# Early query products, key copies and row scaling at the layer boundary of an eight-layer linear-attention stack

## The chip, the cores and the metric

The kernel runs on one core of one Trainium2 chip. The metric is device time in microseconds (us) of one execution. A core has five engines that run their own queues in order and wait for each other through semaphores: PE (matrix products; its weight loads are listed as PEld), DVE (elementwise work with reductions), ACT (activation functions and copies), POOL (elementwise work), and SP (here it issues the weight loads from memory). PE writes its results into eight banks of accumulator memory (PSUM), from which DVE and ACT read.

## The reference

`x` is 512 tokens by 512 features. Three blocks are added to it: cross-attention over 8192 context tokens, a stack of eight linear-attention layers, and an expert layer. All times of this change lie in the stack (about 1234 to 2510 us of the profiled execution). One of its layers, cut to what matters:

```
q = x @ Wq + bq;  k = x @ Wk + bk;  v = x @ Wv + bv
Q = elu(q) + 1;   K = elu(k) + 1
KV = sum over tokens of K * v;   Ksum = sum over tokens of K
V = Q * KV / (Q * Ksum + 1e-6)
x = layernorm(gelu(V @ Wo + bo) + x) * ln1_s + ln1_b
h = gelu(x @ Wf1 + bf1)
x = layernorm(gelu(h @ Wf2 + bf2) + x) * ln2_s + ln2_b
```

Everything is computed in 32-bit floating point.

## The kernel before, in words

**Layout.** The 512 tokens are four tiles of 128 rows (t = 0 to 3). `cur` holds x with tokens on the partitions, `curT` the same with features on the partitions, as the products need it. A layer's queries and values are eight products of 128 features by 512 tokens each (`chunks` 0 to 3 are queries, 4 to 7 values). The keys, like the hidden layer, are computed in a form with seven half products in place of eight (`Seven`); its first two (`p12`) need only the first half of the tokens, `take` reads them from their bank (an ACT copy, L748, and a DVE addition, L749) and hands the first half of the keys to `keys_taken`, which applies elu. `token_sums` (L720 to L723) makes sums of the two halves of the tokens, three on DVE and one on POOL, and `rest` does the other products of the keys (`p5`, `p6`, `p7`, `p4`, `p3`) with DVE additions between (`add6`, L782, is the first, and `p3` reuses the bank that `add6` reads).

**elu.** `elu1` makes elu(x)+1 in five operations: for queries ACT's relu of the negative (L621) and relu (L625), both read from the bank, ACT's exponential (L626), a POOL operation (L627) and DVE's sum (L628). For keys the first is DVE's L623.

**The layer boundary.** The last layernorm of a layer ends tile by tile (`finish`): ACT's gelu, DVE's addition and moments, a root by Newton steps of one column each (L82), and DVE's normalization (L929). Tiles 2 and 3 come last, one closely behind the other. For each tile `turn` transposes the normalized rows on PE (L944) and ACT copies them scaled and shifted into `curT` (L946, four copies of 128x128). `affine` scales and shifts the rows into `cur` (L937, L938), on DVE for tiles 0 and 1 and on POOL for tiles 2 and 3. In the first layer `transpose_into` (L594, L595) takes the place of `turn`.

`features` runs at the start of the next layer, and PE's order in it is written out by hand: the keys' first products and query products 0 and 1 for the first half of the tokens; the transposes of tile 2; query product 2 for the first half; the transposes of tile 3; query products 0 and 1 for tile 2, then for tile 3, and product 2 for the second half; `rest`; and the other five products. The early products 0 to 2 stand in one bank each (`held`), a bank having room for all 512 tokens. `done` hands a product to elu: for the early ones first the half 0 to 255, then the half 256 to 511.

**What sets the order.** PE's order is that of the program text. The other engines' order is made by a scheduler when the program is built, which also places the waits; `tc.issue_after(x)` keeps what is recorded under it behind x in that order. Accesses to one bank by PE and another engine are kept apart by waits even where they touch different columns.

**Rows.** Each layer needs six rows of parameters in copies for all partitions (`row`, loaded by ACT's queue, L986). They stand in nine buffers, so rows 1 and 2 of a layer go where rows 4 and 5 of two layers before stood (the scale and shift of `affine` at the boundary, R_S2 and R_B2), and are loaded a layer early, at that boundary.

Of the kernel before, what the change touches and what calls it, by code (L numbers as in the profile page):

```python
# [11 lines left out]
ALU = mybir.AluOpType  # L12
# [7 lines left out]
T = 512  # L20
# [25 lines left out]
R_BO, R_S1, R_B1, R_BF2, R_S2, R_B2 = range(6)  # L46
# [8 lines left out]
def perceiver_kernel(  # L55
# [3 lines left out]
    nc = tc.nc  # L59
# [58 lines left out]
    def normalize(dst, src, n, eps, roots=None):  # L118
        mv, r = roots or (moments(src, n), None)
        if r is None:  # L120
            r = rsqrt_of(mv[:, :, 1], n, eps)
        for i in range(n):
            last = nc.vector.tensor_scalar(
                dst[:, i, :], src[:, i, :], mv[:, i, 0:1], r[:, i : i + 1], ALU.subtract, ALU.mult
            )
        return last
# [204 lines left out]
    while min(met) < NCHUNK:  # L331
        p = k % NPAIR
# [192 lines left out]
    last = -1  # L525
    for u, n in enumerate(size):
# [6 lines left out]
        for i in range(n):  # L533
            d = end[u] + 1 + i * span // n // 2
            at(d, late_exponentials if d in end[-3:] else exponentials, u, i)
            last = max(d + 1, first)
# [32 lines left out]
    def attention_weights(l):  # L569
        return [weights(big, m[l], f"{n}{l}") for m, n in ((wk, "wk"), (wq, "wq"), (wv, "wv"), (wo, "wo"))]  # L570
# [19 lines left out]
    def transpose_into(dst, src, t, space, tag):  # L590

        pt = space.tile([P, DC, P], F32, tag=tag, name="pt")
        for dc in range(DC):
            nc.tensor.transpose(pt[:, dc, :], src[:, dc * P : (dc + 1) * P], ident)  # L594
        return nc.scalar.copy(dst[:, :, t * P : (t + 1) * P], pt)  # L595

    with ExitStack() as s_:
# [9 lines left out]
        H = T // 2  # L607
# [23 lines left out]
        def feature(ps, w, c0, xT, t0=0, n=T):  # L631
            for dc in range(DC):
                nc.tensor.matmul(  # L633
                    ps[:, t0 : t0 + n], w[:, dc, c0 : c0 + P], xT[:, dc, t0 : t0 + n],
                    start=(dc == 0), stop=(dc == DC - 1),
                )

        def features(k7, chunks, xT, turns, done, normed):

            held = {}

            def product(i, t0=0, n=T):
                if t0 == 0:
                    held[i] = mm.tile([P, T], F32, tag="mm", name="ps")
                feature(held[i], *chunks[i], xT, t0, n)

            if 1 in turns:
                for p in range(2):  # L650
                    k7.p12(p, 0, P, False)
                turns[1]()
                product(0, 0, P)
                for p in range(2):
                    k7.p12(p, P, P, False)
                product(0, P, P)
            else:
                for p in range(2):
                    k7.p12(p, 0, H, False)
                product(0, 0, H)  # L660
            product(1, 0, H)
            turns[2]()
            with tc.issue_after(normed.ins) if normed else nullcontext():
                for p in range(2):
                    k7.take(p)
            product(2, 0, H)
            turned = turns[3]()
            for t in range(2):
                k7.token_sums(t)
            with tc.issue_after(turned.ins):  # L670
                for i in range(3):
                    done(i, held[i], 0, H)
            for t in (2, 3):
                for i in range(2):
                    product(i, t * P, P)
            product(2, H, H)
            with tc.issue_after(turned.ins):
                for i in range(3):
                    done(i, held[i], H, H)
            k7.rest((0, 1))  # L680
            for i in range(3, len(chunks)):
                product(i)
                done(i, held[i], 0, T)
# [230 lines left out]
        def finish(ps, old, bias, t, eng, g=None):  # L914

            if g is None:
                g = gpool.tile([P, D], F32, tag="g", name="g")
                nc.vector.tensor_tensor(g, ps, bias, ALU.add)
            nc.scalar.activation(g, g, AF.Gelu_apprx_tanh)  # L919
            nc.vector.tensor_tensor(g, g, old[:, t, :], ALU.add)  # L920
            mv = small.tile([P, 1, 2], F32, tag="mv1", name="mv")
            st = small.tile([P, 6], F32, tag="st", name="st")
            nc.vector.bn_stats(st, g)
            nc.vector.bn_aggr(mv[:, 0, :], st)
            r = rsqrt_of(mv[:, :, 1], 1, 1e-6)
            if eng is None:
                return g, mv[:, 0, 0:1], r
            if eng is nc.vector:
                last = nc.vector.tensor_scalar(g, g, mv[:, 0, 0:1], r, ALU.subtract, ALU.mult)  # L929
            else:  # L930
                n = small.tile([P, 1], F32, tag="nmr1", name="nmr")
                last = nc.vector.scalar_tensor_tensor(n, mv[:, 0, 0:1], -1.0, r, ALU.mult, ALU.mult)
                nc.scalar.activation(g, g, AF.Identity, bias=n, scale=r)
            return g, last

        def affine(dst, g, scale, shift, eng=nc.vector):
            eng.tensor_tensor(dst, g, scale, ALU.mult)  # L937
            eng.tensor_tensor(dst, dst, shift, ALU.add)  # L938

        def turn(dst, g, t, c_scale, c_shift):  # L940

            pt = acc.tile([P, DC, P], F32, tag="acc", name="pt")
            for dc in range(DC):
                nc.tensor.transpose(pt[:, dc, :], g[:, dc * P : (dc + 1) * P], ident)  # L944
            for dc in range(DC):
                last = nc.scalar.activation(  # L946
                    dst[:, dc, t * P : (t + 1) * P], pt[:, dc, :], AF.Identity,
                    bias=col[:, c_shift + dc : c_shift + dc + 1], scale=col[:, c_scale + dc : c_scale + dc + 1],
                )
            return last  # L950
# [11 lines left out]
        cur = cpl.tile([P, TT, D], F32, tag="cur", name="cur0")  # L962
        curT = cpl.tile([P, DC, T], F32, tag="curT", name="curT0")
        last = None
        for t in range(TT):
            with tc.issue_after(last.ins) if t else nullcontext():
                last = normalize(cur[:, t : t + 1], x_sb[:, t : t + 1], 1, 1e-5, rooted.get(t))
        s_.enter_context(tc.manual_schedule(engines={nc.tensor.engine}))
        transpose_into(curT, cur[:, 0, :], 0, acc, "acc")
        turns = {t: lambda dst=curT, src=cur[:, t, :], t=t: transpose_into(dst, src, t, acc, "acc") for t in (1, 2, 3)}  # L970

        def keys_of_layer(w_k, xT):

            sw = [hpool.tile([P, 2, 2, P], F32, tag="h", name="sw") for _ in range(4)]
            k7 = Seven([(w_k, ac * P) for ac in range(DC)], xT, sw, None, None, None)
            for p in range(2):
                k7.weight_sums(p, (1, 2, 3, 4))
            return k7

        for l in range(NL):  # L980
            w_k, w_q, w_v, w_o = ahead if l else first[0]
            w_1, w_2 = hidden_weights(l) if l else first[1]
            row = []
# [71 lines left out]
            k7 = k7 if l else keys_of_layer(w_k, curT)  # L1055
            k7.sx = [hpool.tile([P, 2, H], F32, tag="h", name="sx") for _ in range(4)]
            k7.tiles, k7.out = keys_tiles, keys_taken
            features(k7, [(w, ac * P) for w in (w_q, w_v) for ac in range(DC)], curT, turns, taken, last if l else None)


# [3 lines left out]
            gs = {}  # L1064
# [9 lines left out]
            turns = {t: lambda dst=midT, g=gs[t], t=t, c=c1: turn(dst, g, t, *c) for t in (1, 2, 3)}  # L1074
# [54 lines left out]
            for p in range(2, NF // 2):  # L1129
# [13 lines left out]
                last = s7.p4(p)  # L1143
# [12 lines left out]
            def next_sums(t):  # L1156
                def f(q):
                    if q + 4 < back.N:
                        back.token_sums(t, q + 4)
                    elif t == 0 and l + 1 < NL:  # L1160
                        back.token_sums(2, q + 4 - back.N)
                return f

            cur = cpl.tile([P, TT, D], F32, tag="cur", name="cur")
# [11 lines left out]
            for t in (0, 2):  # L1176
                if t:
                    ahead = attention_weights(l + 1)
                g = back.products(t, row[R_BF2], between if t else lambda q: None, next_sums(t))
                for i in range(2):  # L1180
                    gs[t + i], last = finish(None, mid, None, t + i, nc.vector, g[i])
                with tc.issue_after(last.ins):
                    for i in (1, 0) if t else (0, 1):
                        affine(cur[:, t + i, :], gs[t + i], row[R_S2], row[R_B2], nc.gpsimd if t else nc.vector)
            turns = {t: lambda dst=curT, g=gs[t], t=t, c=c2: turn(dst, g, t, *c) for t in (2, 3)}
            k7 = made[0]

# [266 lines left out]
```

## Time and profile before

| what | us |
|---|---|
| median of three runs (lowest, highest) | 2622.29 (2621.86, 2625.03) |
| the profiled execution | 2622.8 |
| its span (first to last instruction) | 2621.0 |
| PE busy | 2510.6 |
| DVE, POOL, ACT busy | 1767.2, 1416.8, 1199.8 |
| early query products of a boundary restart (L633), seven boundaries | 1413.16, 1577.76, 1741.99, 1906.03, 2069.98, 2233.89, 2397.86 |

A line of the timeline has the start and the duration, the engine, the source line, the operation, output<-input by the program's names, the shape and a count, and in brackets the idle time before it with what ended it. In a list of waits a line says who waited, for whom, the total, the number of times and the longest. "PEclk", or the granted clock, is the share of PE's full clock that the chip granted. Engines overlap: an engine's busy time is no part of a sum, and only what PE waits for, or does slower, sets the end where PE is busy 96% of the span.

### The profile page before, as it was taken

To read this page: it belongs to the slowest core of one execution; us is meant where nothing else is said; L and a number is where in the kernel's file an instruction comes from. 1 tells how busy PE (TensorE), PEld (TensorE's weight loads), DVE (VectorE), ACT (ScalarE), POOL (GpSimd) and SP (SyncE) were. 2 spreads that over 40 slices of the span, in tenths; PEclk is the share of its full clock that TensorE was granted. 3 is DMA by queue.
4 is the path that set the end of the run, shared out by engine and by line. 5 is a ranking of instruction groups with operands and counts; after the bars stand their busy time and mean duration, and the time that the engine had idled before them with its cause. 6 is when DMAs were issued, how large, how long until landed. Compare 5 with 4: busy or idle time off the path is not lost.

```text
span 2621.0 us, 32785 instructions
## 1 busy us (share of the span) xinstructions
PE 2510.6 (96%) x10936; PEld 1508.8 (58%) x10936; DVE 1767.2 (67%) x3786; ACT 1199.8 (46%) x2263; POOL 1416.8 (54%) x1606
## 2 busy tenths in 40 slices
PE   8999999999999999988999999999999999899998
PEld 4433333433433343334687786877868778587763
DVE  4466767767777677886666676676766767667664
ACT  3466656656666566662514416244162441624413
POOL 0255656665666656763365554655546555475512
PEclk9999999999999999999999999999999999999999
DMA  4111011111111111101423232232322323222235
GB/s 136 46 43 46 26 39 41 41 41 41 41 41 41 37 36 41 29 20 61 164 73 109 78 100 77 73 109 73 104 77 73 109 72 106 77 73 97 65 118 189
DMA packets 98377, 187.43 MB, mean 72 GB/s; under 512 B 10336, under 2 KB 10464, under 8 KB 98208
## 3 DMA queue, kind: packets, MB, share of 16 engines
q1 hardware_dynamic: 88496, 167.29, 20.0%
q10 hardware_dynamic: 8688, 15.94, 1.8%
q0 software_dynamic: 1024, 2.10, 0.2%
q8 instruction: 87, 1.43, 0.2%
q14 instruction: 82, 0.67, 0.1%
HBM read 162.22 MB, written 1.05 MB: 62 GB/s over the span
## 4 chain that ended last, share of the span: by engine, by line
PE 76%; DVE 11%; ACT 6%; issue 4%; POOL 2%; DMA 1%; SPq 0%; DVEq 0%; POOLq 0%; ACTq 0%
PE pb L862 14%; PE pw L727 11%; PE ps L633 7%; PE pv L259 7%; PE ps L727 7%; PE pk L230 7%; PE po L455 7%; PE pc L374 6%; PE po L1070 4%; DVE sc L434 3%; ACT sc L377 2%; ACT sc L435 1%; PE pt L218 1%; PE pf L956 1%; DVE mx L383 1%
## 5 line engine op out<-in xcount | busy, mean ns | idle before, releaser
L445 POOL TENSOR_TENSOR es<-es,sc 128x1024 f32<-128x1024 f32 x222 | 525.3, 2366 | 113.2 <-ACT sc L435 102.3
L383 DVE TENSOR_TENSOR mx<-pc,mx 128x512 f32<-128x512 f32 x448 | 283.0, 683 | 192.2 <-ACT sc L377 192.0
L435 ACT ACTIVATE sc<-sc 128x1024 f32<-128x1024 f32 x272 | 288.1, 1063 | 242.7 <-DVE sc L434 231.6
L377 ACT COPY sc<-pc 128x512 f32<-128x512 f32 x544 | 284.4, 599 | 91.4 <-PE pc L374 78.1
L434 DVE TENSOR_TENSOR sc<-sc,mbc 128x1024 f32<-128x1024 f32 x272 | 319.0, 1207 | 3.7 <-PE mbc L411 2.2
L374 PE MATMUL pc<-qT,k 64*128 64x512 f32 x1088 | 288.2, 621 | 2.9 <-ACT v L265 1.3
L455 PE MATMUL po<-sc,v 128*64 128x512 f32 x1088 | 265.1, 608 | 0.2 <-DVE mx L383 0.2
L230 PE MATMUL pk<-xn,wkv 128*128 128x512 f32 x544 | 253.0, 609 | 7.1 <-ACT v L265 2.9
L259 PE MATMUL pv<-wkv,xn 128*128 128x512 f32 x544 | 249.6, 602 | 6.3 <-DVE sin L241 3.3
L374 PEld LDWEIGHTS pc<-qT,k 64*128 64x128 f32 x1088 | 101.0, 186 | 183.9 <-issue 77.9
L1081 ACT ACTIVATE h<-h,col 128x256 f32<-128x256 f32 x192 | 103.8, 575 | 220.5 <-DVE h L795 151.0
L919 ACT ACTIVATE g<-g 128x512 f32<-128x512 f32 x64 | 39.8, 628 | 319.6 <-DVE g L879 218.8
L230 PEld LDWEIGHTS pk<-xn,wkv 128*128 128x128 f32 x544 | 99.8, 192 | 149.1 <-issue 107.0
L259 PEld LDWEIGHTS pv<-wkv,xn 128*128 128x128 f32 x544 | 98.4, 190 | 140.8 <-issue 106.7
L727 PE MATMUL pw<-curT,cur 128*128 128x256 f32 (+1 forms) x896 | 177.2, 350 | 0.0
L633 PE MATMUL ps<-curT,wq 128*128 128x128 f32 (+2 forms) x584 | 130.5, 386 | 45.0 <-ACT r L625 45.0
L627 POOL TENSOR_SCALAR m<-m 128x256 f32<-128x256 f32 (+1 forms) x104 | 106.5, 1034 | 117.3 <-ACT m L626 115.1
L714 POOL TENSOR_TENSOR cur<-w 128x256 f32<-128x256 f32 x128 | 93.5, 741 | 135.2 <-DVE g L920 84.8
L727 PEld LDWEIGHTS pw<-curT,cur 128*128 128x128 f32 x896 | 150.2, 190 | 16.8 <-DVE curT L720 0.2
L828 POOL TENSOR_TENSOR sh<-h 128x128 f32<-128x128 f32 x120 | 82.8, 690 | 133.1 <-PE pb L862 128.8
L455 PEld LDWEIGHTS po<-sc,v 128*64 128x64 f32 x1088 | 67.8, 137 | 145.9 <-issue 123.5
L633 PEld LDWEIGHTS ps<-curT,wq 128*128 128x128 f32 x584 | 101.0, 220 | 64.6 <-ACT r L625 47.1
(252 smaller groups left out, 4712.9 us busy)
## 6 DMA issues: line engine op xcount, KB each, us to landing
w<-in_wf SPq DMA_DIRECT2D x64, 1024.0 KB, 5.2
k<-cos SPq DMA_DIRECT2D x272, 64.0 KB, 2.0
cb<-in_cx SPq DMA_DIRECT2D x62, 256.0 KB, 3.2
row<-in_rows ACTq DMA_DIRECT2D x48, 256.0 KB, 4.7
f<-in_f SPq DMA_DIRECT2D x10, 1024.0 KB, 5.5
tg<-in_trig SPq DMA_DIRECT2D x16, 512.0 KB, 3.9
wk<-in_wk SPq DMA_DIRECT2D x8, 1024.0 KB, 5.1
wq<-in_wq SPq DMA_DIRECT2D x8, 1024.0 KB, 5.3
```

The costliest lines, as they stand in the source:

```text
L230: nc.tensor.matmul(pk, wkv[:, 0, dc, j * P : (j + 1) * P], xT[b, dc], start=(dc == 0), stop=(dc == DC - 1))
L259: nc.tensor.matmul(pv, xT[b, dc][:, t * P : (t + 1) * P], wkv[:, 1, dc, :], start=(dc == 0), stop=(dc == DC - 1))
L374: nc.tensor.matmul(pc[h], k_sb[b, p][hs, o : o + P], qT[hs, p, :], start=True, stop=True)
L377: copied[0] = nc.scalar.copy(sc[:, h, :], pc[h])
L383: behind[0] = nc.vector.tensor_tensor(mx[u][:, h, :], pc[h], mx[u][:, h, :], ALU.max)
L434: nc.vector.tensor_tensor(sc, sc, mbc[u], ALU.subtract)
L435: nc.scalar.activation(sc, sc, AF.Exp)
L445: nc.gpsimd.tensor_tensor(es[u], es[u], sc, ALU.add)
L455: nc.tensor.matmul(po[u][h * HD : (h + 1) * HD, :], v_sb[b, p][:, t * P + h * HD : t * P + (h + 1) * HD], scores[u, i][:, h, :], start=(i ...
L633: nc.tensor.matmul(ps[:, t0 : t0 + n], w[:, dc, c0 : c0 + P], xT[:, dc, t0 : t0 + n], start=(dc == 0), stop=(dc == DC - 1),)
L727: nc.tensor.matmul(ps, lhs[:, k], rhs[:, k], start=(k == 0), stop=(k == 1))
L862: nc.tensor.matmul(ps[i], lhs, rhs, start=(q == 0 and i in (1, 2, 6, 5, 4)), stop=(q == self.N - 1 and i in (1, 2, 7, 3, 4)),)
```

## The change

Three edits, two in `features` and one where the layers call `affine` (with `affine` now returning its last operation):

1. Query products 0 to 2 go to elu once, over all 512 tokens, when all their products are recorded, and no more in two halves.
2. The keys' `take` is recorded under `issue_after` of the third tile's last copy into `curT`, so that these copies come first.
3. The scaling of each pair of tiles is chained: the first `affine` stands behind the normalization of the second tile of the pair, and each further one behind the one before it, so that POOL takes tile 3, then tile 2.

```diff
@@ features
             product(1, 0, H)
-            turns[2]()
+            turned = turns[2]()
             with tc.issue_after(normed.ins) if normed else nullcontext():
-                for p in range(2):
-                    k7.take(p)
+                with tc.issue_after(turned.ins):
+                    for p in range(2):
+                        k7.take(p)
             product(2, 0, H)
             turned = turns[3]()
             for t in range(2):
                 k7.token_sums(t)
-            with tc.issue_after(turned.ins):
-                for i in range(3):
-                    done(i, held[i], 0, H)
             for t in (2, 3):
                 for i in range(2):
                     product(i, t * P, P)
             product(2, H, H)
+
             with tc.issue_after(turned.ins):
                 for i in range(3):
-                    done(i, held[i], H, H)
+                    done(i, held[i], 0, T)
@@ affine
             eng.tensor_tensor(dst, g, scale, ALU.mult)
-            eng.tensor_tensor(dst, dst, shift, ALU.add)
+            return eng.tensor_tensor(dst, dst, shift, ALU.add)
@@ the layers
                     gs[t + i], last = finish(None, mid, None, t + i, nc.vector, g[i])
-                with tc.issue_after(last.ins):
-                    for i in (1, 0) if t else (0, 1):
-                        affine(cur[:, t + i, :], gs[t + i], row[R_S2], row[R_B2], nc.gpsimd if t else nc.vector)
+                scaled = last
+                for i in (1, 0) if t else (0, 1):
+                    with tc.issue_after(scaled.ins):
+                        scaled = affine(
+                            cur[:, t + i, :], gs[t + i], row[R_S2], row[R_B2], nc.gpsimd if t else nc.vector
+                        )
```

In the built program PE's and SP's instructions stand in the same order as before. On ACT, at a boundary, the order after the gelus was: the two bank copies L748, the first key's relu, tile 2's copies, the table load and the keys' exponentials, tile 3's copies, then the queries' elus in six parts, with the loads of rows 1 and 2 between them. It is now: tile 2's copies, the first bank copy, the load of row 1, the first key's relu, the second bank copy, the table load and the keys' exponentials, tile 3's copies, the load of row 2, then the queries' elus in three parts. The load of row 1 waits for POOL's multiplication of tile 2's rows (L937). At the last boundary there are no rows left to load; there ACT takes both bank copies and the first of tile 3's four copies before the first relu.

## The prediction

> **What bounds the kernel now.** I read the page's busy table first, then what the matmul engine (PE) waits for in the layers (1250 to 2560 us), then the timeline of one layer boundary, then the granted clock over that boundary.
>
> ```profile
> PE 2510.6 (96%) x10936; PEld 1508.8 (58%) x10936; DVE 1767.2 (67%) x3786; ACT 1199.8 (46%) x2263; POOL 1416.8 (54%) x1606
> ```
> ```profile
> PE ps L633 <- ACT r L625: 45.0, 9, 6.2
> PE pt L944 <- ACT g L933: 5.5, 8, 0.7
> PE pt L944 <- DVE g L929: 1.9, 7, 0.3
> ```
>
> PE is the bound: in the eight layers it waits 52 us in all, and 45.0 of them at one place, the early query products (L633) behind the relu that reads their bank (L625): seven boundaries of 6.16 us, and 1.9 us at the first layer's start. The timeline between layers 1 and 2:
>
> ```profile
> 1567.47 1.28 POOL L937 TENSOR_TENSOR cur<-g,row 128x512 f32<-128x512 f32 x1 [12.84 <-DVE g L929]
> 1567.56 1.21 DVE L82 SCALAR_TENSOR_TENSOR ny<-nt,ny 128x1 f32<-128x1 f32 x1
> 1568.80 1.31 DVE L82 SCALAR_TENSOR_TENSOR nt<-ny,vh 128x1 f32<-128x1 f32 x1
> 1568.34 0.60 PE L944 MATMUL pt<-ident,g 128*128 128x128 f32 x4
> 1570.94 0.66 PE L944 MATMUL pt<-ident,g 128*128 128x128 f32 x4 [0.28 <-DVE g L929]
> 1571.25 0.51 ACT L625 ACTIVATE r<-kf,col 128x256 f32<-128x256 f32 x1 [5.79 <-DVE kf L749]
> 1571.67 1.49 ACT L946 ACTIVATE curT<-pt,col 128x128 f32<-128x128 f32 x4
> 1573.17 1.28 ACT L626 ACT_TABLE_LOAD   x1
> 1575.49 1.48 ACT L946 ACTIVATE curT<-pt,col 128x128 f32<-128x128 f32 x4
> 1577.22 0.48 ACT L625 ACTIVATE r<-ps,col 128x256 f32<-128x256 f32 x1
> 1577.76 7.29 PE L633 MATMUL ps<-curT,wq 128*128 128x128 f32 x40 [6.16 <-ACT r L625]
> ```
> ```profile
> 1571.17:1574.58 3.41, 0.43 (x4) 1.00 0.00 0
> 1574.58:1578.00 3.42, 0.24 (x1) 0.50 0.00 0
> 1578.00:1581.41 3.41, 3.41 (x17) 0.50 0.06 20
> 1581.41:1584.82 3.41, 3.41 (x25) 1.00 0.45 136
> ```
>
> Three things are to be seen. The third tile's transposes end at 1568.94, yet its copies (L946) start at 1571.67: ACT stands at a relu that waits for DVE. Two one-column DVE operations take 1.21 and 1.31 us, exactly while POOL's 1.28 us scaling runs (the same operations take 0.16 and 0.22 without it). And the stall is dearer than its 6.16 us: in the last table (stretch; length, PE busy, granted clock) the clock is halved one mostly idle window of 3.41 us later and is whole again only at 1581.41, so PE works 3.65 us at half rate and loses 1.8. Over the seven boundaries that half-rate work is 4.40, 3.65, 3.26, 3.06, 2.95, 2.88 and 6.16 us, so 13.2 us are lost beside the stalls.
>
> **The change, part by part** (times of this boundary, line numbers of before; the built order of each engine's instructions is read from the two programs).
>
> PE's order and SP's are unchanged. *The bank read once*: the products for the third and fourth tile wait only for the copies of curT. *Scaling after the norm*: POOL starts when the fourth tile is normalized; DVE's two operations fall to 0.38 together, so L929 ends 1.21+1.31-0.38 = 2.14 us earlier, at 1568.76. PE's gap before the transposes goes; they end near 1570.9. *Copies ahead*: L946 of the third tile runs 1568.97 to 1570.46, so its 16 products (0.118 each at full clock: 32 took 3.79 in layer 0) run 1570.9 to 1572.8.
>
> The fourth tile sets the rest. The change moves the load of a row (`row`, L986) on ACT's queue ahead of the first relu, and it now waits for POOL's multiplication of the third tile, which POOL does after the fourth tile's two operations. Behind it on ACT stand both keys' elus and, after them, the fourth tile's copies, for which PE waits. That such a wait blocks ACT shows at 1552.70: ACT was idle 15.22 us, issued this load once DVE's L879 was done, and copied 0.44 us later. POOL: three operations of 1.28 with 0.05 to 0.08 between, from 1568.84, end at 1572.8. DVE's token sums beside them are not seen together in this trace; nearest, POOL's 256-wide L722 takes 0.78 to 0.99 beside DVE's L720 instead of L714's 0.73. So 0 to 0.84 (two sums of 0.42) is added; I take 0.5: 1573.3. Then load 0.44, relu 0.42, copy 0.37, table 1.30, exponential, relu and exponential 1.02, four copies 1.5: 5.05 us. The last copy ends at 1578.4 (1576.97 before), the first at 1577.4, and PE idles 4.6 us instead of 6.16. After the last copy PE needs 10 products of 0.12 and 8 of 0.215, so the keys' remaining products start at 1581.35 at full clock; before, 1577.76+3.79+1.72 = 1583.27. **1.9 us at each of six boundaries: -11.4.**
>
> The Trainium skill (SBUF — State Buffer, Who interferes with whom) calls the port pair of VectorE and GpSimd an exclusive lock: who starts first holds it for the whole instruction. By that rule both sums would hold POOL up, 0.84, and the sum would be 2 us worse; the 1.21 and 1.31 us rows agree with the lock.
>
> *The clock.* 4.6 us of idling still holds a window that is idle enough: windows with 1.46 us or less of work are followed by a halved one, windows with 1.73 or more are not (one of 2.10 excepted). By phase, PE then works 2.9 to 6.3 us at half rate, of which 0.3 hides behind copies that it awaits: 1.2 to 2.85 us per boundary. I take 2.2, so 13 for six, where before lost 10.1: **+3** (-3 to +7).
>
> *The last boundary* has no row to load. ACT is not held; the table load ends at 1573.6, the second exponential waits for POOL's port until 1574.7, the copies end at 1576.2, the rest starts at 1579.1: -4.2. PE idles 2.4 us, which halves the clock in some 6 phases of 10, for 1.5: 0.9 instead of 3.1. **-6.4.**
>
> *The first layer's start*: no POOL scaling and no row in the way; both waits (1.42 and 0.47) and their pipeline refill go, and the rest starts at 1253.6 instead of 1255.79: **-2.2.**
>
> *At nothing*: three elus of 512 columns for six of 256. They end later: with 1.3 to 1.5 us for POOL's 512 columns and 0.75 for DVE's, the third query is out at 1587.1 and DVE's L782 pair at 1587.85; PE asks for that bank at 1588.2. Cover 0.35 us, and whatever exceeds it is paid at each boundary. The exponentials for the output product had 3.5 us to spare (y ready 1606.7, asked for at 1610.3); they come 2.3 us earlier, PE 3 at most. The first two tiles' scalings, now one after the other on DVE, lie beside products that run to 1561. cur, later on POOL, is first read at 1615.7.
>
> Sum, on the profiled execution's own 2622.8 us (1.8 outside its span; 0.5 above the median of the runs): 2622.8 - 2.2 - 11.4 + 3 - 6.4 = **2605.8 us**.
>
> **Rivals.**
>
> *The clock takes it back* (0.16). Successive boundaries lie 164.2, 164.0, 163.95 and 163.9 us apart, close to 48 windows of 3.413 = 163.84: whoever arrives early waits longer for the next edge. If the period locks there again, six periods bring 6 x 0.28 = 1.7, the start and the first boundary 4.1, the last 5: 2612. For it: an idle time of 4.6 leaves room for the 5 to 6 us at half rate that this needs. Against: a period without its half-rate loss is 162.4 now (164.23 - 1.82) and would be 160.5; a period of 163.84 then needs 6.7 us at half rate, and at most 6.3 fit. With 0.5 us less gained per layer it fits. The Trainium skill (TensorE: Matmul & The Clock Gate, What's actually happening) has a free-running window of 3413 ns, which these rows show.
>
> *The gate no longer closes* (0.07). If POOL and DVE do not collide and the phases are kind, the half-rate loss of 13.9 goes: 2592. Against: 4.6 us is far over one window.
>
> *The wait only moves* (0.12): the fourth tile's copies come 1.9 us later than I say, PE's gap keeps its length with another releaser: some 2620, the first start alone gained.
>
> *Slower* (0.11): POOL. Its 128-wide L828 went from 0.46 to 0.90 us beside DVE's two-input additions (1549 to 1552). If its 512-wide operations double too, to 2.5, the awaited one ends at 1576.5, the last copy at 1581.6, the rest starts at 1584.6: 1.3 late, with some 8 us of idling and 1.2 more at half rate. Six times 2.5, less some 3 for the first start and the last boundary: 2635. It decides from 2.2 us per operation (0.94 over 1.28, three operations, six boundaries: 17 us). Against: these operations took 1.26 to 1.29 us beside L749 and L623, which waited instead.
>
> **Numbers.** Forecast 0.54, its own range 2598 to 2612 from POOL's 0 to 0.84 and the clock's bounds. Faster is 0.54+0.16+0.07 = 0.77, within 0.2% (5 us, about what a measurement here can tell from none) 0.12, slower 0.11. 2593 to 2621 leaves out the slower rival, most of the open gate and the far side of the wait that only moves.
>
> **What would show it.** Right: L633 waits for curT (L946) and not for L625; no one-column L82 over 1 us at a boundary; the fourth tile's L937 first on POOL; ACT idle before its row load until POOL's third operation; query elus 128x512; 4 to 5 us of idling at six boundaries and about 2.4 at the last. Wrong: POOL's scalings over 2 us, a new wait of PE for DVE's L782, or no ACT wait at the load (then faster still).

## The result, and the profile after

The changed kernel takes 2604.37 us (median of four runs, 2603.30 to 2604.95) beside 2622.47 for the kernel before (four runs, 2621.86 to 2625.03): a ratio of 0.9929, 95% interval 0.9911 to 0.9946. The profiled execution took 2604.4 us with a span of 2602.6; the forecast was 2605.8, from 2593 to 2621. From here on lines of `after` are meant where nothing else is said: one less than in the kernel before up to `affine` and behind it (L945 is the copy into `curT` that was L946, L985 the row load that was L986). In the experiments they shift by a few more.

The page's busy table, and what PE waits for in the layers (1250 to 2560 us):

```profile
PE 2513.4 (97%) x10936; PEld 1513.2 (58%) x10936; DVE 1746.6 (67%) x3762; ACT 1187.6 (46%) x2191; POOL 1413.3 (54%) x1582
```
```profile
PE ps L633 <- ACT curT L945: 27.0, 7, 4.1
PE pt L943 <- ACT g L932: 5.5, 8, 0.7
```

The wait for the relu that reads the bank (45.0 us) is gone; in its place PE waits for the fourth tile's copies, 4.1 us at six boundaries and 2.4 at the last, 27.0 in all. The timeline of the same boundary as before, between layers 1 and 2:

```profile
1564.91 0.55 DVE L928 TENSOR_SCALAR g<-g,mv,ny 128x512 f32<-128x512 f32 x1
...
1565.54 1.30 POOL L936 TENSOR_TENSOR cur<-g,row 128x512 f32<-128x512 f32 x1 [14.06 <-DVE g L928]
1565.69 1.50 ACT L945 ACTIVATE curT<-pt,col 128x128 f32<-128x128 f32 x4 [6.01 <-PE pt L943]
...
1566.92 1.33 POOL L937 TENSOR_TENSOR cur<-cur,row 128x512 f32<-128x512 f32 x1
...
1567.22 1.31 DVE L720 TENSOR_TENSOR sx<-curT,sx 128x256 f32<-128x256 f32 x1
...
1568.21 1.48 POOL L936 TENSOR_TENSOR cur<-g,row 128x512 f32<-128x512 f32 x1
1568.45 0.41 DVE L748 TENSOR_TENSOR kf<-kf,ps 128x256 f32<-128x256 f32 x1
1568.78 1.19 DVE L722 TENSOR_TENSOR sx<-curT,sx 128x256 f32<-128x256 f32 x1
1569.72 0.33 ACTq L985 DMA_DIRECT2D row<-in_rows  x1
...
1570.10 0.51 ACT L625 ACTIVATE r<-kf,col 128x256 f32<-128x256 f32 x1 [2.65 <-DVE sx L722]
...
1570.88 1.28 ACT L626 ACT_TABLE_LOAD   x1
...
1573.20 1.48 ACT L945 ACTIVATE curT<-pt,col 128x128 f32<-128x128 f32 x4
...
1573.70 6.66 PE L633 MATMUL ps<-curT,wq 128*128 128x128 f32 x24 [4.09 <-ACT curT L945]
```

Three things are to be seen. The third tile's copies now come first on ACT (1565.69), as the change says. Then ACT stands idle for 2.65 us. The list names DVE's token sum as releaser, but the row load was issued at 1569.72, 0.03 us after POOL's third scaling ended (1568.21 + 1.48), and the relu follows 0.38 later; the addition for which the relu itself waits (L748) was done at 1568.86. And behind the relu stand the table load, the exponentials and only then the fourth tile's copies, at 1573.20.

The granted clock around two successive boundaries (stretch; length, PE busy, granted clock):

```profile
1569.44:1572.85 3.41, 0.16 (x2) 1.00 0.22 77
1572.85:1576.26 3.41, 2.56 (x12) 0.50 0.33 77
1576.26:1579.67 3.41, 3.41 (x12) 0.50 0.00 0
```
```profile
1733.28:1736.69 3.41, 0.16 (x1) 1.00 0.32 110
1736.69:1740.10 3.41, 3.41 (x17) 0.50 0.15 49
1740.10:1743.51 3.41, 3.41 (x17) 1.00 0.00 0
```

In both a nearly idle window is followed by a halved one. Where PE restarts 0.85 us into the halved window, that window is busy for 2.56 us only and a second halved one follows; where it restarts just ahead of it, the window is full and the clock returns after one. In the kernel before, the clock stayed halved behind a halved window with 2.75 us of work (2397.19 to 2400.61) and returned behind one with 2.88 (2233.35 to 2236.77). The six boundaries take turns: one window, two, one, two, one, two.

PE's instructions are the same in both kernels, so the same instruction's start can be compared from end to end. After minus before, in us:

```
ahead of the stack                +1.73
behind the first layer's start    -0.40   (-2.13)
behind boundaries 1 to 6          -3.29  -4.70  -7.14  -8.33  -10.65  -11.81   (-11.41)
behind the last boundary          -17.02  (-5.21)
end of PE's work                  -17.93  (-0.91)
```

The +1.73 arises ahead of the stack, in cross-attention, which the change does not touch: 0.7 of it in the first 16 us, and 1.3 because after has a halved stretch of 6.83 us (at 316.7) and before one of 3.41 (at 376.5). The -0.91 lies behind the stack; its cause was not followed.

### The profile page after: what moved, and what is told of

Its sections match the earlier page's. It is cut to its first block, busy times and chain, and to the rows that moved or that the text cites. A ratio compares the mean times of both kernels' runs of the same rounds, so it can differ in the third digit from the quotient of the medians.

```text
span 2602.6 us, 32659 instructions
## 1 busy us (share of the span) xinstructions
PE 2513.4 (97%) x10936; PEld 1513.2 (58%) x10936; DVE 1746.6 (67%) x3762; ACT 1187.6 (46%) x2191; POOL 1413.3 (54%) x1582
## 4 chain that ended last, share of the span: by engine, by line
PE 71%; DVE 9%; POOL 7%; issue 7%; ACT 5%; DMA 0%; ACTq 0%; SPq 0%; POOLq 0%; DVEq 0%
PE pw L726 11%; PE pb L861 9%; PE ps L633 7%; PE ps L726 7%; PE pv L259 7%; PE pk L230 6%; PE po L455 6%; PE pc L374 6%; DVE sc L434 4%; PE po L1069 4%; ACT sc L377 2%; ACT sc L435 1%; POOL es L445 1%; PE pt L218 1%; PE pf L955 1%
## 5 line engine op out<-in xcount | busy, mean ns | idle before, releaser
L627 POOL TENSOR_SCALAR m<-m 128x512 f32<-128x512 f32 (+1 forms) x80 | 102.0, 1287 | 75.9 <-ACT m L626 75.1
L861 PE MATMUL pb<-tw,sh 128*128 128x256 f32 x540 | 136.3, 380 | 0.0
```

The costliest lines, as they stand in the source:

```text
L861: nc.tensor.matmul(ps[i], lhs, rhs, start=(q == 0 and i in (1, 2, 6, 5, 4)), stop=(q == self.N - 1 and i in (1, 2, 7, 3, 4)),)
```

## Experiments

All times are medians of four runs (ten for part 3 alone) beside the kernel before on the same chip (2620.9 to 2622.1 in these comparisons); brackets hold the ratio to the kernel before with its 95% interval. The changed kernel's 2604.37 stood beside 2622.47, so a difference from it carries up to 1.5 us of that. The parts of the change are called 1 (banks read once), 2 (third tile's copies ahead of the keys' take) and 3 (scalings chained).

**One part, and all but one.** Part 1 alone (in the kernel before):

```diff
-            with tc.issue_after(turned.ins):
-                for i in range(3):
-                    done(i, held[i], 0, H)
...
-                    done(i, held[i], H, H)
+                    done(i, held[i], 0, T)
```

> The kernel before with one part of the change: the three early queries are read once, behind all products that fill their banks. The third tile's copies stay where they were, between the first key's relu and the table load, and POOL's scalings are not held back. Theory A (what is left of PE's stall in the changed kernel, 4.1 us at six boundaries, is made by ACT standing at the load of a row that waits for POOL's third scaling): here that load stands behind the fourth tile's copies, so these end where they ended before, 1.0 us earlier than in the changed kernel on one scale; PE waits twice, some 1.6 and 1.4 us, and a boundary gains 3.4 us against before: 2622.5 - 2.2 - 7 x 3.4 = about 2597, less up to 10 us if two short waits no longer halve the clock. Theory B (all three parts are needed, the earlier transposes above all): 2606 to 2615. That the bank is not the cause: 2620.

Measured: 2585.19 (0.9858, 0.9843 to 0.9872). One part alone gives twice the gain of the three together. From its list of PE's waits:

```profile
PE ps L633 <- ACT curT L943: 13.7, 14, 1.4
```

PE waits twice per boundary, for the third and the fourth tile's copies, never over 1.4 us, and no window at a boundary is halved. Theory B falls. Theory A fits, with more gain than the 2597 named first, as the clock's part came in full; but this run alone does not tell the load from the order of the copies. The load is also not where it was expected: at the second boundary it stands at 1567.13, ahead of the fourth tile's copies (1568.08), but the scaling for which it waits had ended at 1564.86, and ACT goes on without a gap.

Part 2 left out (of the changed kernel):

```diff
-                with tc.issue_after(turned.ins):
-                    for p in range(2):
-                        k7.take(p)
+                for p in range(2):
+                    k7.take(p)
```

> The changed kernel without the second part: the keys are taken as soon as the fourth tile of the layer below is normalized, and not behind the third tile's copies; banks read once, scalings in a chain as in the changed kernel. ACT's order is then relu, third tile's copies, table load, exponentials, fourth tile's copies, with no load of a row ahead of them. Theory A: the ACT queue is freed from POOL, the fourth tile's copies end 2 to 3 us earlier than in the changed kernel, and the stall of 4.1 us falls below 2.5: 2588 to 2598. Theory B (the copies ahead are what shortens the stall): slower than the changed kernel's 2604.4, some 2606 to 2612.

Measured: 2579.06 (0.9837, 0.9822 to 0.9851), 25 us faster than the changed kernel. Theory B falls; theory A has the direction and too small a size, as its range ended at 2588. From its timeline, ACT at the same boundary, and PE:

```profile
1561.75 0.51 ACT L625 ACTIVATE r<-kf,col 128x256 f32<-128x256 f32 x1 [3.66 <-DVE kf L747]
...
1562.16 1.49 ACT L944 ACTIVATE curT<-pt,col 128x128 f32<-128x128 f32 x4
...
1563.67 1.28 ACT L626 ACT_TABLE_LOAD   x1
...
1565.44 0.33 ACTq L984 DMA_DIRECT2D row<-in_rows  x1
...
1565.99 1.48 ACT L944 ACTIVATE curT<-pt,col 128x128 f32<-128x128 f32 x4
1566.48 4.16 PE L633 MATMUL ps<-curT,wq 128*128 128x128 f32 x24 [0.96 <-ACT curT L944]
```

The relu sets the third tile's copies back by some 0.4 us, which PE does not feel, as it is still at the third query and the fourth tile's transposes. The row load is not ahead of the relu. It stands between the second relu and the last exponential, still ahead of the fourth tile's copies, and costs nothing there: that exponential starts 0.39 us behind its relu, as in the kernel before (0.40).

Part 3 left out (the scalings as before, 1 and 2 as in the change):

> The first two parts of the change without the third: banks read once, third tile's copies ahead of the keys' elus, but the scalings as in the kernel before (first the third tile, as soon as it is normalized). Theory (part two is what costs, through two loads of rows on ACT's queue that wait for POOL and through DVE, where token sums now stand ahead of the key's addition; part three only eases both): in this order the loads stand ahead of the third tile's copies and wait for POOL's scaling of the fourth tile, so PE waits in two places, some 3.5 us more per boundary than with the bank alone (2585), and a halved clock comes back: 2608 to 2620, slower than the changed kernel. Rival (the three parts are nearly independent, part two costs 25 and part three brings 6): 2610. Rival (part two is only bad together with the chain on POOL, which makes its load wait for the third operation and not for the first): 2585 to 2592.

Measured: 2609.82 (0.9955, 0.9940 to 0.9970). From its timeline:

```profile
1571.59 0.33 ACTq L985 DMA_DIRECT2D row<-in_rows  x1
...
1571.98 1.15 ACT L945 ACTIVATE curT<-pt,col 128x128 f32<-128x128 f32 x3 [9.72 <-POOL cur L936]
```

One load stands ahead of the third tile's copies, as expected, the other ahead of the last of them, but both the theory and the rival of independent parts allow this time; only the rival that part 2 harms through the chain alone falls.

Part 3 alone:

> The kernel before with the third part alone: POOL scales the last two tiles one after the other, the fourth first, from when the fourth is normalized; queries still read from their banks in two halves, with PE's products for the last tiles behind the first reading. Theory (two things set a boundary: the bank, and how soon the fourth tile and the keys get through DVE): DVE's two one-column operations fall from 1.21 and 1.31 to 0.2 us, transposes and key additions come 1 to 2 us earlier, ACT's chain with them, and the stall of 6.16 us stays near 5 to 6 at an earlier place: 2608 to 2614. Rival (with the bank still in the way the chain brings nothing, or the keys' token sums beside POOL take it back): 2618 to 2624.

Measured: 2622.91 (1.0003, 0.9994 to 1.0013): nothing. The theory falls and the rival holds. From its timeline:

```profile
1577.52 1.83 POOL L627 TENSOR_SCALAR m<-m 128x256 f32<-128x256 f32 x2
...
1579.22 0.47 ACT L621 ACTIVATE m<-ps,ncol 128x256 f32<-128x256 f32 x1 [1.87 <-DVE kf L628]
...
1580.12 7.45 PE L633 MATMUL ps<-curT,wq 128*128 128x128 f32 x40 [6.50 <-ACT r L625]
```

The transposes do come earlier, but POOL's part of the keys' elu (L627) stands behind the four chained scalings, and the first reading of a query's bank (L621) waits for the keys' sums behind it, as it writes one of the two buffers of `m` that the keys' elus still hold. What DVE gained is lost on POOL, and PE idles 6.50 us instead of 6.16.

So part 1 brings 36 us (2621 to 2585); part 3 nothing without it and 6 with it (to 2579, intervals that just overlap); part 2 costs 25 in both cases (2585.2 to 2609.8, 2579.1 to 2604.4). Part 2 was not run without part 1.

**Why part 2 costs.** The row loads first. They are needed only a layer later, so they can be issued well behind the boundary (changed kernel; `weighed_last` is the last exponential of `weighed` in the layer before):

```diff
-                nc.scalar.dma_start(out=rt, in_=rows[l, i].partition_broadcast(P))
+                with tc.issue_after(weighed_last.ins) if l > 1 else nullcontext():
+                    nc.scalar.dma_start(out=rt, in_=rows[l, i].partition_broadcast(P))
```

> The changed kernel with the loads of the rows for layer l+1 issued only behind the last exponential of layer l's keys' weighing (they are read 100 us and more later), so that ACT meets no load that waits for POOL ahead of the first key's relu. Nothing else differs. Theory A: ACT goes on when the first key is added up (1568.86 at the second boundary) and not when POOL is done (1569.7); copies of the fourth tile 1.2 us earlier, stall 2.9 instead of 4.1: 6 x 1.2 = 7.4 less, and up to 7 more from the clock: 2590 to 2598. Rival (DVE's key additions, stretched by POOL, set the relu; the load only waited beside them): 2602 to 2605. Rival (the clock's windows hold the period at 47 and 48 windows in turn and take the gain back): 2602 to 2605 with a shorter stall but more work at half rate.

Measured: 2590.16 (0.9878, 0.9861 to 0.9894), 14.2 less than the changed kernel. Theory A holds, and the gain stays: the clock did not take it back. Its timeline:

```profile
1562.98 0.74 DVE L748 TENSOR_TENSOR kf<-kf,ps 128x256 f32<-128x256 f32 x2
1563.43 0.51 ACT L625 ACTIVATE r<-kf,col 128x256 f32<-128x256 f32 x1 [0.56 <-DVE kf L748]
...
1566.77 5.41 PE L633 MATMUL ps<-curT,wq 128*128 128x128 f32 x22 [2.38 <-ACT curT L945]
```

ACT now waits 0.56 us for the keys' addition in place of 2.65; PE's stall is 2.4 us, and each of boundaries 2 to 6 has one halved window, the first and the last none. Next, DVE's token sums behind the keys' additions, on top of this:

> The changed kernel with the row loads later (as in the run with that change alone, 2590) and, besides, DVE's token sums of the first and third tile behind the two additions of the keys. The third tile's copies are still ahead of the keys' elus. Theory A (what is left between 2590 and the 2579 of the kernel without the copies ahead is DVE's order: two or three token sums, stretched to 1.2 to 1.3 us each beside POOL, stand ahead of the key's addition for which ACT's relu waits): PE's wait falls from 2.4 to about 1, no halved window, 2578 to 2582. Rival (the order on ACT itself, four copies of 1.5 us ahead of relu and table load, sets it): 2588 to 2591, with a wait of 2.4 us that stays.

Measured: 2587.78 (0.9869, 0.9854 to 0.9883), 2.4 less, with overlapping intervals; PE's stall is 2.2 us. Theory A falls and the rival, whose range began at 2588, holds: what is left is ACT's own order, which the last experiment of this section changes. ACT in this run:

```profile
1562.27 1.50 ACT L947 ACTIVATE curT<-pt,col 128x128 f32<-128x128 f32 x4 [6.00 <-PE pt L945]
...
1564.52 0.91 ACT L625 ACTIVATE r<-kf,col 128x256 f32<-128x256 f32 x2 [0.22 <-DVE kf L749]
1565.45 1.28 ACT L626 ACT_TABLE_LOAD   x1
...
1567.87 1.49 ACT L947 ACTIVATE curT<-pt,col 128x128 f32<-128x128 f32 x4
```

ACT has hardly a gap here. Copies, relus, table load and exponentials follow each other, and the last copies come when all that is done.

**The clock by itself.** The stall filled with useless work (changed kernel, layers 1 to 7; not shown: `product` also keeps the bank that it already has):

```diff
             for t in (2, 3):
                 for i in range(2):
                     product(i, t * P, P)
+                if t == 2 and normed:
+                    for _ in range(2):
+                        product(2, 0, H)
```

> The changed kernel with useless work for PE in the stall: at the seven boundaries the first half of the third query's product (1.72 us) is computed twice more, with the same result, between the products of the third tile and those of the fourth. PE's order is otherwise the same, and 3.44 of the 4.1 us idle are filled. Theory of the clock (a window of 3.41 us that is mostly idle halves the clock for one or two windows): no halved window is left at the boundaries, and the half-rate work of the six boundaries (3.41, 5.98, 3.41, 5.80, 3.41, 5.75, in sum 27.8 us) and of the last (3.41) loses nothing: 13.9 + 1.7 saved, 1.0 paid at the last boundary, whose stall is only 2.42: 2604.4 - 14.6 = about 2590. Rival (the halving comes from something else at a boundary, or returns as power is drawn): 2604 to 2606.

Measured: 2591.99 (0.9882, 0.9867 to 0.9897), 12.4 less than the changed kernel although PE does 24 us more work (seven times 3.44). From its timeline, the third tile's products with the useless ones behind them, and the fourth tile's:

```profile
1566.70 5.41 PE L633 MATMUL ps<-curT,wq 128*128 128x128 f32 x32
1572.77 4.15 PE L633 MATMUL ps<-curT,wq 128*128 128x128 f32 x24 [0.66 <-ACT curT L948]
```

The fourth tile's products take 4.15 us in place of 6.66, and no boundary has a halved window. The theory of the clock holds; 2.2 us of the 14.6 expected did not show. By the starts of the same instructions, each of the six boundaries gained 0.3 to 0.5 us less than expected and the last some 0.5 more; why stays open.

**Towards a better kernel.** From the 2579 kernel, work moved into its last waits (halves of the keys' fifth and sixth product computed early):

> The best kernel so far (no copies ahead, 2579) with work moved into PE's last two waits of a boundary: of the keys' products with sums, the halves that need only the first and third tile's token sums are computed early, those of the fifth product between the third and the fourth tile's query products, those of the sixth behind the third query; the second halves follow. Each 256-wide product becomes two of 128. Theory (PE is the bound, and its waits of 0.96 for the fourth tile's copies and 0.63 for DVE's token sums are all that is left at a boundary): up to 1.4 us at each of seven boundaries and some at the first layer: 2569 to 2574. Rival (the fourth tile's copies only come later relative to the work, or ACT's next elus become the wait, as q's banks are read later): 2576 to 2582.

Measured: 2577.07 (0.9825, 0.9809 to 0.9842), which can't be told from 2579. The rival holds, with another releaser than it named; DVE and PE later at this boundary:

```profile
1578.47 0.69 DVE L628 SCALAR_TENSOR_TENSOR qf<-m,r 128x512 f32<-128x512 f32 x1 [2.09 <-POOL m L627]
1579.08 0.41 DVE L791 TENSOR_TENSOR kf<-kf,pw 128x256 f32<-128x256 f32 x1
```
```profile
1579.64 1.97 PE L736 MATMUL pw<-curT,sw 128*128 128x256 f32 x8 [1.09 <-DVE kf L791]
```

The stall moved 10 us on, to the bank that `add6` (L791 here) reads, which now stands behind the third query's elu. Then the opposite of part 2's order: from the 2579 kernel, the first halves of the keys' elus go behind the fourth tile's copies (`take` with False does copy and addition, and leaves the elu to `out`).

```diff
                 for p in range(2):
-                    k7.take(p)
+                    k7.take(p, False)
...
             turned = turns[3]()
+            with tc.issue_after(turned.ins):
+                for p in range(2):
+                    k7.out(2 * p, k7.o[p][0], 0, H)
```

> The kernel without the copies ahead (2579) with the first halves of the keys' elus moved behind the fourth tile's copies; the keys' copies and additions stay early. The planner then puts two loads of rows on ACT's queue between the third and the fourth tile's copies, and they wait for POOL's third and fourth scaling. Theory (a load that waits on ACT's queue costs what it waits, whatever stands behind it): the fourth tile's copies start with the end of POOL's fourth scaling, about 1 us later than in the 2579 kernel, though no elu is ahead of them: PE waits about 2 us, 2585 to 2592, and some halved windows. Rival (an issue of a load behind a short wait costs ACT nothing that counts): 2566 to 2572.

> The same with the loads of the rows later, so that nothing that waits for POOL stands ahead of the fourth tile's copies: third tile's copies, fourth tile's copies, then relu, table load and exponentials of the keys. Theory (what is left of the boundary's stall is ACT's order, 1.28 us of table load and 1.8 of elus between the two sets of copies): the fourth tile's copies start when its transposes are done, 2.2 us earlier; PE's waits of 0.96 for them and of 0.63 for the token sums go: 7 x 1.6 = 11 less: 2566 to 2571. Rival (the keys' elus, which come later, or the bank that the third query's elu frees, become the wait): 2574 to 2582.

Measured: 2583.10 (0.9852, 0.9837 to 0.9866) with the loads in the way, 2563.96 (0.9778, 0.9762 to 0.9795) without them. Both lie 2 us below what their theories gave, and far from their rivals. ACT with the loads in the way, then ACT and PE without:

```profile
1566.06 1.74 ACTq L988 DMA_DIRECT2D row<-in_rows  x2
...
1567.85 1.50 ACT L948 ACTIVATE curT<-pt,col 128x128 f32<-128x128 f32 x4 [4.11 <-POOL cur L940]
```
```profile
1560.68 5.46 PE L633 MATMUL ps<-curT,wq 128*128 128x128 f32 x40
1560.88 1.50 ACT L948 ACTIVATE curT<-pt,col 128x128 f32<-128x128 f32 x4 [0.66 <-PE pt L946]
...
1562.27 0.52 ACT L625 ACTIVATE r<-kf,col 128x256 f32<-128x256 f32 x1
```

Two loads that nobody needs for a layer hold ACT for 4.11 us and cost 19 us in all; PE waits up to 2.2 us for the copies behind them, and four boundaries have a halved window. Without them the products of the third and fourth tile run as one block of 40 and PE waits for nothing at the boundary. This kernel beats both: 58 us below the kernel before, 40 below the changed one.

One more number at this boundary shows how far ACT's queue holds back what PE waits for: from the end of the fourth tile's normalization to the first of its copies (in the run with the rows later, to the second; one had slipped ahead).

```
before, 1, 3, 1+3                       4.60 us
1+2                                     7.22
1+2+3 (the changed kernel)              7.74
1+2+3, rows later                       6.26
1+2+3, rows later, token sums behind    5.82
1+3, keys' elus behind                  5.85
1+3, keys' elus behind, rows later      2.39
```

It does not order the times by itself. Where the banks are still read in two halves it says nothing (4.60 at 2621 and 2623). Among the others, 2.39 and 4.60 go with 2564 to 2585, and 7.22 and 7.74 with 2610 and 2604, but 5.82 goes with 2588 and 5.85 with 2583: at the last boundary, which has no loads, the first stays at 5.84 and the second falls to 2.39.

## Why the prediction was right, point by point

The time was right, and so was the chain of causes; one term of the sum was too small, one too large, and two shifts lay outside it. That the forecast is only 1.4 us off is in part luck: the terms missed by 3.0 (six boundaries, forecast -8.4 with the clock) one way and by 1.2 (the last) and 0.8 (outside the sum) the other.

- *PE's wait for the bank goes; the wait is then for the fourth tile's copies.* Right: 45.0 us for L625 are gone, 27.0 for L945 stand there.
- *POOL chained, DVE's one-column operations short.* Right: the last two Newton operations took 0.22 and 0.16, 0.38 together, and POOL's scalings 1.30, 1.33, 1.48 and 1.32. Nothing doubled, so the slower rival had no ground.
- *ACT stands at the row load until POOL's third scaling, and so holds the fourth tile's copies.* Right, and here are its parts, from the end of the fourth tile's normalization: third scaling done 4.5 forecast, 4.2 measured; first copy 8.1 and 7.7; last copy done 9.6 and 9.2; PE idle 4.6 and 4.10. The row-later run shows that this load was the cause.
- *Collision of DVE and POOL.* The 0.5 us were put on the wrong engine. POOL's third scaling lost 0.2; DVE's operations beside the scalings took 1.31, 1.19 and 1.35 us in place of 0.42, 0.43 and 0.37. The Trainium skill (SBUF — State Buffer, Who interferes with whom) has who blocks decided by the order of issue; the prediction worked out only the case in which DVE starts first. Here POOL's scaling had started 0.30 us ahead of the sum at 1567.22, and the sum ended 0.28 behind it, 1.31 us after its start: the trace agrees.
- *Six boundaries, -11.4 + 3.* Mis-sized: -11.41 with the clock in it. The clock's term was near, +3 forecast: half-rate work of 3.41, 5.98, 3.41, 5.80, 3.41 and 5.75 us loses 13.9 where before lost 10.1, so +3.8. What was too small is the 1.9 us per boundary, which was (11.41 + 3.8) / 6 = 2.5: the stall was 0.5 shorter than forecast.
- *Last boundary, -6.4.* Measured -5.2. The idle time was 2.42, as forecast, but the window did halve (3.41 us of work, 1.7 lost), and only 0.9 had been counted for a chance of 6 in 10. That is 0.8 of the miss; the other 0.4 is the gain without the clock, 3.8 in place of 4.2.
- *First layer's start, -2.2.* Measured -2.13.
- *At nothing: wider elus.* Right; PE never waits for L781 or for the exponentials behind. How thin that cover of 0.35 us is, this trace shows (L781 ends at 1585.14, PE's products for that bank start at 1585.37), and in the run with the early halves PE waits there for 1.09 us.
- *Outside the sum:* +1.73 ahead of the stack, most of it from where the clock's windows fall, and -0.91 behind it, not explained. The forecast's terms sum to -17.0; the same terms measured to -2.13 - 11.41 - 5.21 = -18.75, and with these two to -17.93.
- *The clock takes it back.* Wrong as put: the period does not lock at 48 windows. Successive restarts lie 161.71, 162.83, 161.61, 162.75 and 161.58 us apart, so two periods take some 324.4, close to 95 windows of 3.413 (324.3): the kernel alternates between one halved window and two.

What the prediction did not see is that the three parts pull against each other. It priced the row load on ACT's queue in full, but as part of a sum that came out negative, and never asked what parts 1 and 3 would give without it.

## What to carry to other kernels

Price each edit of a change against the others, not only their sum: here one edit brought 36 us and another gave 25 back, and the sum looked like a success. A load whose buffer was not yet free held up all that stood behind it on ACT's queue here (for 2.65 us, and in another order 4.11); if nobody needs such a load soon, tie its issue to a later instruction (14 us in one kernel here, 19 in another). On the engine that feeds the bottleneck, put the copies that the bottleneck waits for ahead of table loads and of work with slack, for all tiles: for all it gave 2564 here, for none 2579, for one of two 2588, each with no load in the way.

## What the hardware showed that was not expected

- Filling a stall with useless products made the kernel 12.4 us faster, since PE's clock stayed whole: the fourth tile's block of products fell from 6.66 to 4.15 us.
- A halved window in which PE is busy 2.56 of 3.41 us (2.75 in the kernel before) does not bring the clock back; one with 2.88 or a full one does. So a stall of 4.1 us cost 1.7 or 2.9 us more, by where it fell.
- DVE additions of 256 columns that read two operands beside POOL's scalings took 1.19 to 1.31 us in place of 0.42, and L623, which reads one such operand, took 1.35 in place of 0.37.
